# Normalised rows turned by VectorE and DMA instead of TensorE, and row stores issued by ScalarE, in a four-layer float32 block

## The chip, the cores and the metric

The kernel runs on one core of a Trainium2 chip. The metric is the device time of one execution in microseconds. Three executions of the kernel before took 2465.59, 2468.93 and 2472.80 us; the median, 2468.93 us, is the time that the changed kernel is compared with. Engines are named TensorE (PE in the profile), VectorE (DVE), ScalarE (ACT), GpSimd (POOL) and SyncE (SP, which only issues DMAs here).

## The reference

Four layers in a row work on x, 4 batches of 512 rows of 512 numbers, all float32. Each layer adds its result to x:

```python
x = x + attn_a(layernorm(x), Wq, Wk, Wv, Wo)   # "first attention"
x = x + ffn(layernorm(x), w1, w2, w3)          # first feed-forward
x = x + attn_b(layernorm(x), mxfp4 weights)    # "second attention"
x = x + ffn(layernorm(x), w1, w2, w3)          # second feed-forward
```

`layernorm` subtracts the mean of a row and divides by its deviation. First attention has 16 query heads of 128 in 4 groups, each with one key and value head. Its output is half a causal softmax attention with rotary positions, half a gated linear recurrence (`S = S * exp(g) + k v`, with g from the keys). The feed-forward is `sigmoid(n @ q(w1).T) * (n @ q(w2).T) @ q(w3).T`, where n is the normalised x and q rounds weights to -1, 0 and 1. What matters here: every layer begins with normalised rows, and TensorE needs them with the 512 features on partitions, so each block of 128 rows by 512 features has to be turned.

## The kernel before

x stays in SBUF as 16 tiles `xs` of 128 rows. A row block's normalised form is made in `layernorm_steps` (line 123), a Python generator that is advanced from the outer loops, a piece at a time: moments by VectorE (lines 130 to 133), scales (135 to 145, one power on GpSimd), then for each of four row blocks the scaled rows `xn` (line 160, VectorE), four 128x128 transposes by TensorE into one PSUM bank (line 165), and a `sink` that copies the bank to SBUF: ScalarE alone in first attention (line 372), ScalarE and VectorE as a high and a low half in the other layers (`halved`, lines 174 to 177, with `split`, 118 to 121).

First attention (`first_attention_gentle`, line 311) runs 73 steps, one for each 128-row chunk of each of 16 groups (4 batches by 4 head groups) and a few to fill and drain. `step(n)` (line 552) works on several chunks at once, named u to z for chunks n-2 to n+3:

- `A` projects the queries, `B` makes their softmax with decay, turns 32x32 blocks by VectorE (line 461, tile `turned`, one buffer) and stores them to DRAM (line 463); one step later `L` reads them back with the blocks exchanged (line 470), so that queries arrive turned without TensorE.
- `C` turns the rotated queries by TensorE, `D(0)` to `D(3)` make the scores of four heads and their softmax; after the fourth, the turned rows are stored (line 503). `E` reads them back (line 509) at the start of the next step, `own` and `F` form the output, and `G` adds it to x, two steps after the chunk's `D`.
- `part` does the same for the keys of the next group over its four steps p = 0 to 3; `decays` (line 407) sends three one-partition rows `ends` to another place by DMA (line 420).
- `quantise` rounds the feed-forward weights beside all this, a piece at two places of each step.
- `normalise` (line 369) of the next batch is advanced in three of the four steps of the group before it is needed, at up to four places of a step.

In steps 0 to 63 TensorE runs in program order (`manual_schedule`, line 624). The other engines and the rest of the program are ordered by the framework's planner, which puts on each engine what is ready first by its own cost model. `in_place` pins an instruction behind whatever was written before it for the same engine; all these stores and loads are pinned, on SyncE's queue. Each engine then executes its list strictly in order, and a DMA issue that has to wait holds up everything behind it on that engine.

The feed-forward (`feed_forward`, line 1077) loads 11 weight blocks, then for each batch computes 11 pairs of projections (lines 1090 to 1104) and four row blocks of output (1105 to 1112). The next batch's rows are advanced from the loop over blocks (line 1102). Batch 0 of the first feed-forward is normalised during the last steps of first attention (`ahead(50, 0)`, line 1128).

Of the kernel before, what the change touches and what calls it, by code (L numbers as in the profile page):

```python
# [9 lines left out]
F32 = mybir.dt.float32  # L10
# [3 lines left out]
F32R = mybir.dt.float32r  # L14
AF = mybir.ActivationFunctionType
ALU = mybir.AluOpType
# [3 lines left out]
P = 128  # L20
B, S, C = 4, 512, 512
NC = S // P
NK = C // P
# [51 lines left out]
def hybrid_block(ctx: ExitStack, tc: tile.TileContext, a: dict, out: bass.AP):  # L75
# [42 lines left out]
    def split(hi, lo, src, engine=nc.vector):  # L118

        nc.scalar.copy(hi, src)  # L120
        engine.tensor_tensor(lo, src, hi, ALU.subtract)

    def layernorm_steps(b, sink, tag="tp", apart=False, place=lambda i: i):


# [9 lines left out]
        def scales(at):  # L135
# [9 lines left out]
            nc.vector.tensor_tensor(r, r, t, ALU.mult)  # L145

        if not apart:
            for c in range(NC):
                moments(c)
                if c == 1:  # L150
                    yield
            scales(slice(0, NC))
        for c in range(NC):
            if apart:
                moments(c)
                scales(slice(c, c + 1))
            else:
                yield
            xn = lnp.tile([P, C], F32, tag="xn", name="xn", bufs=1)
            nc.vector.tensor_scalar(xn, xs[b * NC + c], mv[:, c, 0:1], rstd[:, c : c + 1], ALU.subtract, ALU.mult)  # L160
            if not apart:
                yield
            tp = bank(tag, [P, NK, P])
            for k in range(NK):
                t = nc.tensor.transpose(tp[:, k, :], xn[:, k * P : (k + 1) * P], ident)  # L165
                if k == 0:
                    place(t)
            sink(c, tp)
# [5 lines left out]
    def halved(pool, b, **kw):  # L174

        halves = [pool.tile([P, NK, S], F32R, tag=f"xn{n}", name=f"xn{n}") for n in ("hi", "lo")]
        return halves, layernorm_steps(b, lambda c, tp: split(*(h[:, :, c * P : (c + 1) * P] for h in halves), tp), **kw)

    def whole(pool, b):
# [130 lines left out]

    def first_attention_gentle(base, extra):

# [5 lines left out]
        with ExitStack() as st:  # L318
# [49 lines left out]

            def normalise(b, apart=False):
                xnT = base.tile([P, NK, S], F32, tag="xnhi", name="xnT")  # L370
                xnTs[b] = xnT
                return layernorm_steps(b, lambda c, tp: nc.scalar.copy(xnT[:, :, c * P : (c + 1) * P], tp), apart=apart)

            class Group:
# [32 lines left out]
                def decays(self):  # L407
# [11 lines left out]
                    for c in range(NC - 1):  # L419
                        nc.sync.dma_start(self.ends[:, c : c + 1], self.down[P - 1 : P, c, :])  # L420
                    n = self.g * B + self.b
# [23 lines left out]
            class Chunk:  # L445
# [9 lines left out]
                def B(self):  # L455
                    c = self.c
                    qd = one.tile([P, HG, D], F32, tag="qd", name="qd")
                    softmax_decayed(qd, self.q_t, lambda h: self.k.down[:, c, :])

                    turned = one.tile([P, 4, HG, 32], F32, tag="turned", name="turned")  # L460
                    nc.vector.transpose(turned.rearrange("p q h t -> p h q t"), qd.rearrange("p h (q j) -> p h q j", q=4))
                    self.queries = dram.tile([P, HG * D], F32, tag="queries", name="queries", bufs=3)
                    in_place(nc.sync.dma_start(self.queries, turned.rearrange("p q h t -> p (q h t)")))
                    self.qr = two.tile([P, HG, D], F32, tag="qr", name="qr")
                    rotate(self.qr, self.q_t, turn[:, c : c + 1, 0:1, :], turn[:, c : c + 1, 1:3, :])

                def L(self):
# [16 lines left out]
                def D(self, h):  # L484
# [15 lines left out]
                    nc.vector.transpose(self.turned.rearrange("p (q h x) -> p q h x", q=4, h=HG)[:, :, h, :], pr.rearrange("p (q x) -> p q x", q=4))  # L500
                    if h == HG - 1:
                        self.passed = dram.tile([P, 4 * HG * P], F32, tag="passed", name="passed", bufs=3)[:, : 4 * HG * 32 * n]
                        in_place(nc.sync.dma_start(self.passed, self.turned))

# [42 lines left out]

            for _ in normalise(0, apart=True):
                pass
            ln = iter(())  # L550
            groups[0] = Group(0, 0)
            def step(n):
                nonlocal ln
                m, p = divmod(n + 7, NC)
                at = lambda i: chunks.get(n + i) if n + i < last else None
                if p == 0 and (m + 2) % KV == 0 and (m + 2) // KV < B:
                    load((m + 2) // KV)
                if (m + 1) % KV == 0 and (m + 1) // KV < B:
                    if p == 1:
                        ln = normalise((m + 1) // KV)  # L560
                    if p > 1:
                        next(ln)
                u, v, w, x, y, z = (at(i) for i in range(-2, 4))
# [4 lines left out]
                if n > -4:  # L568
                    next(quant, None)
                if w:  # L570
                    w.E()
                part(m, p, 0)
# [5 lines left out]
                if x:  # L578
                    x.D(0)
                if z and n > -2:  # L580
                    z.A()
# [3 lines left out]
                if x:  # L585
                    x.D(1)
                if p:
                    next(ln, None)
                if z:
                    z.B()  # L590
                if x:
                    x.D(2)
                if p > 1:
                    next(ln, None)
                if w:
# [14 lines left out]
                if x:  # L610
                    x.D(3)
                if n in (-2, *range(NC + 1, last, NC)):
                    groups[max(n // NC, 0)].load_wo()
                if p:
                    next(ln, None)
                if n > -4:
                    next(quant, None)
                for f in extra.get(n, ()):
                    f()

# [6 lines left out]
            for n in range(last, last + 2):  # L627
                step(n)
            assert next(quant, 0) == 0

# [446 lines left out]
    def feed_forward(base, last, first):  # L1077

        with ExitStack() as st:
# [7 lines left out]
            for b in range(B):  # L1087
                ready, steps = halved(base, b + 1, place=in_place) if b + 1 < B else (None, iter(()))
                hid = []
                for f, (w, _) in enumerate(ws):  # L1090
# [10 lines left out]
                    hid.append(halves)  # L1101
                    for _ in range((f > 1) + (f == 2)):
                        next(steps, None)
                    yield b, f
                for c in range(NC):
                    y = bank("mm", [P, C])
                    project(y, lambda i: hid[i // 2][i % 2][:, c * P : (c + 1) * P], lambda i: ws[i // 2][1][:, 0, :], 2 * NF)
                    x = xs[b * NC + c]
                    nc.vector.tensor_tensor(x, x, y, ALU.add)
                    if last:  # L1110
                        nc.sync.dma_start(x_out[b * NC + c], x)
                    yield b, NF + c
                xn = ready

    with banks(mm=2, sc=3, tp=2, pv=1), tc.tile_pool(name="base", bufs=2) as base:
# [11 lines left out]

        first_attention_gentle(base, ahead(50, 0))
        attention = second_attention_exact(base, ahead(-14, 1))
# [64 lines left out]
```

## Time and profile before

| | before |
|---|---|
| median of three runs | 2468.93 us |
| the profiled execution's own time | 2466.74 us |
| its span, first to last instruction | 2464.8 us |
| busy: TensorE, VectorE, ScalarE, GpSimd | 98%, 67%, 49%, 16% |
| first attention, from the traces | about 0 to 1031 us |
| second feed-forward | about 2194 us to the end |
| TensorE transposes of normalised rows (line 165) | 256, of 280 ns mean |
| DMA, mean over the span | 149 GB/s |

Busy is the union of an engine's instructions. Matmuls are pipelined, so a matmul shown with 0.59 us may follow the one before it after 0.43 us; the distance from start to start is what one costs. The granted clock of TensorE is 0.996 of full speed over the span.

### The profile page before, as it was taken

The numbers are of one execution on the slowest core, as the hardware profiler recorded it, in microseconds if no ns is written. First come the engines' busy times: TensorE is split into PE (matmuls) and PEld (weight loads), VectorE is DVE, ScalarE is ACT, GpSimd is POOL, SyncE is SP. The second block draws the span as 40 slices with busy tenths as digits, with TensorE's granted clock in tenths as the row PEclk, the third lists the DMA queues.
The fourth block names the chain that finished last, engine by engine and source line by source line (L and its number), as shares of the span: only waits on it lengthen the run. The fifth ranks groups of instructions, "written<-read, shape, count | busy, mean of one in ns | idle before, by whom it ended". The sixth has DMA issues, their size and how long they took to land.

```text
span 2464.8 us, 28979 instructions
## 1 busy us (share of the span) xinstructions
PE 2425.2 (98%) x8552; PEld 1543.2 (63%) x8552; DVE 1643.5 (67%) x3816; ACT 1210.8 (49%) x3066; POOL 387.6 (16%) x424
## 2 busy tenths in 40 slices
PE   7999999999999999899999999999999999999998
PEld 4555555555555555488876666666666666658887
DVE  5888777878788888355558676667766666663332
ACT  5666666666666665333336455444444444432221
POOL 1222222222122222022224333100000000000000
PEclk9999999999999999999999999999999999999999
DMA  4667776777656664564536777534343435333000
GB/s 137 198 191 204 201 204 182 205 205 201 180 175 192 196 180 149 193 190 129 143 125 169 199 201 200 144 105 128 91 131 87 132 92 144 78 97 121 18 18 19
DMA packets 240616, 367.11 MB, mean 149 GB/s; under 512 B 41664, under 2 KB 126912, under 8 KB 234304
## 3 DMA queue, kind: packets, MB, share of 16 engines
q1 hardware_dynamic: 214192, 305.03, 44.2%
q10 hardware_dynamic: 18576, 34.95, 4.7%
q0 software_dynamic: 7680, 25.17, 3.6%
q8 instruction: 71, 1.16, 0.2%
q14 instruction: 97, 0.79, 0.1%
HBM read 209.53 MB, written 88.34 MB: 121 GB/s over the span
## 4 chain that ended last, share of the span: by engine, by line
PE 86%; DVE 5%; DMA 3%; issue 2%; ACT 1%; SPq 1%; POOL 1%; DVEq 0%; ACTq 0%; POOLq 0%
PE mm L188 44%; PE sc L188 10%; PE sc L890 8%; PE pv L520 5%; PE sc L490 5%; PE pv L924 4%; PE tp L924 4%; PE sc L480 2%; PE tp L364 2%; PE pv L518 1%; SPq L917 1%; DMA block<-blocks 1%; PE tp L165 1%; DMA prT<-turned 1%; DMA wo<-in_Wo 0%
## 5 line engine op out<-in xcount | busy, mean ns | idle before, releaser
L895 ACT ACTIVATE pr<-sc,nm 128x512 f32<-128x512 f32 x256 | 175.9, 687 | 301.6 <-DVE nm L892 258.3
L188 PE MATMUL sc<-xnhi,block 128*128 128x512 f32 x704 | 278.6, 396 | 3.7 <-ACT hT L1097 2.8
L188 PE MATMUL sc<-xnlo,block 128*128 128x512 f32 x704 | 275.4, 391 | 0.0
L890 PE MATMUL sc<-kT,qT 128*128 128x512 f32 x512 | 262.1, 594 | 0.4 <-ACT kT L872 0.4
L188 PE MATMUL mm<-xnhi,w 128*128 128x512 f32 x512 | 254.4, 497 | 0.0
L188 PE MATMUL mm<-wo,oT 128*128 128x512 f32 x512 | 232.2, 596 | 4.4 <-DMA wo<-in_Wo 3.8
L188 PE MATMUL mm<-wq,xnT 128*128 128x512 f32 x512 | 230.9, 594 | 0.1
L892 DVE TENSOR_REDUCE nm<-sc 128x1 f32<-128x512 f32 x256 | 174.9, 683 | 73.4 <-PE sc L890 70.9
L188 PE MATMUL mm<-xnlo,w 128*128 128x512 f32 x512 | 205.8, 402 | 0.0
L912 DVE STREAM_TRANSPOSE turned<-pr 128x512 f32<-128x512 f32 x256 | 173.4, 696 | 36.8 <-ACT pr L902 34.0
L499 ACT ACTIVATE pr<-pr,den 128x128 f32<-128x128 f32 (+3 forms) x256 | 141.5, 557 | 86.3 <-DVE den L498 84.5
L902 ACT ACTIVATE pr<-pr,den 128x512 f32<-128x512 f32 x192 | 138.2, 722 | 82.3 <-DVE den L900 82.1
L345 POOL TENSOR_TENSOR sw<-q_t,turn 128x256 f32<-128x256 f32 x128 | 97.1, 780 | 495.5 <-ACT q_t L453 396.5
L490 PE MATMUL sc<-krT,qrT 128*128 128x512 f32 (+3 forms) x512 | 170.4, 434 | 0.4 <-DVE own L482 0.4
L497 ACT ACTIVATE pr<-sc,nm 128x128 f32<-128x128 f32 (+3 forms) x256 | 132.9, 520 | 64.0 <-DVE nm L494 54.9
L188 PEld LDWEIGHTS mm<-wo,oT 128*128 128x128 f32 x512 | 96.3, 191 | 105.3 <-issue 95.0
L188 PEld LDWEIGHTS mm<-wq,xnT 128*128 128x128 f32 x512 | 96.3, 191 | 105.1 <-issue 98.8
L500 DVE STREAM_TRANSPOSE turned<-pr 128x128 f32<-128x128 f32 (+3 forms) x256 | 128.4, 503 | 46.7 <-ACT pr L499 43.4
L188 PEld LDWEIGHTS sc<-xnhi,block 128*128 128x128 f32 x704 | 132.8, 189 | 33.3 <-ACT hT L1097 4.0
L188 PEld LDWEIGHTS sc<-xnlo,block 128*128 128x128 f32 x704 | 132.8, 189 | 27.8 <-issue 0.7
L520 PE MATMUL pv<-prT,v_t 128*128 128x512 f32 x320 | 148.0, 592 | 0.0
L890 PEld LDWEIGHTS sc<-kT,qT 128*128 128x128 f32 x512 | 95.8, 189 | 81.4 <-issue 63.6
(151 smaller groups left out, 4800.7 us busy)
## 6 DMA issues: line engine op xcount, KB each, us to landing
prT<-turned SPq DMA_DIRECT2D x1024, 64.0 KB, 2.0
w<-exact SPq DMA_DIRECT2D x32, 1024.0 KB, 5.5
wq<-in_Wq ACTq DMA_DIRECT2D x16, 1024.0 KB, 5.3
queries<-turned SPq DMA_DIRECT2D x64, 256.0 KB, 2.8
qdT<-queries SPq DMA_DIRECT2D x256, 64.0 KB, 3.3
wo<-in_Wo ACTq DMA_DIRECT2D x16, 1024.0 KB, 6.1
passed<-turned SPq DMA_DIRECT2D x16, 1024.0 KB, 4.3
prT<-passed SPq DMA_DIRECT2D x64, 256.0 KB, 5.9
```

What stands on the lines that cost most here:

```text
L188: nc.tensor.matmul(acc, lhsT=lhs(k), rhs=rhs(k), start=k == 0, stop=k == n - 1)
L490: nc.tensor.matmul(sc.rearrange("p q (k j) -> p q k j", j=32), lhsT=self.qrT[:, h, :], rhs=self.k.krT.rearrange("p (k q j) -> p q k j", q= ...
L497: nc.scalar.activation(pr, flat, AF.Exp, bias=nm, scale=-1.0, accum_out=den)
L499: nc.scalar.mul(pr, pr, den)
L500: nc.vector.transpose(self.turned.rearrange("p (q h x) -> p q h x", q=4, h=HG)[:, :, h, :], pr.rearrange("p (q x) -> p q x", q=4))
L520: nc.tensor.matmul(acc.rearrange("p h (a t) -> p h a t", a=4), lhsT=self.k.v_t[:, j, :], rhs=self.wts[:, :, :, j, :], start=j == c == 0, s ...
L890: nc.tensor.matmul(sc, lhsT=qTs[u][:, i * P : (i + 1) * P], rhs=kTs[u], start=True, stop=True)
L892: nc.vector.tensor_reduce(nm, sc, AX.X, ALU.max, negate=True)
L895: nc.scalar.activation(pr, sc, AF.Exp, bias=nm, accum_out=den)
L902: nc.scalar.mul(pr, pr, den)
L912: nc.vector.transpose(turns[u][:, :, i, :], pr.rearrange("p (q k) -> p q k", q=4))
L924: nc.tensor.matmul(accs[u].rearrange("p (n t) -> p n t", t=32), lhsT=v_ts[m, j][:, h * D : (h + 1) * D], rhs=prTs[u].rearrange("p a i (k t ...
```

## The change

Three things change, in first attention and in the second feed-forward.

1. Normalised rows of batches 1 to 3 of first attention, of batch 0 of the first feed-forward, and of batches 1 to 3 of the second feed-forward are no longer turned by TensorE. `to_dram` scales the rows, turns their 32x32 blocks by VectorE and stores 256 KB to DRAM; `from_dram` reads them back by four DMAs of 64 KB that exchange the blocks; ScalarE (and VectorE, for the halves) writes them where the layer reads them. In first attention the turned tile shares the one buffer of `B`'s `turned`, and the tile read back shares the one buffer of `xn`.
2. In first attention the stores of queries and of softmax rows and the three `ends` go from SyncE's queue to ScalarE's, at other places: the rows' store after the next step's `D(0)`, the queries' store after `D(3)`. `E` moves from the start of a step to after `D(1)`.
3. Rows of a batch are advanced at two places of every step over seven steps instead of up to four places over three, starting a few steps earlier; x of a batch is loaded one group earlier. In the second feed-forward the generator is advanced once for every block and output row block.

```diff
+    def to_dram(turned, c, rows):
+        nc.vector.transpose(turned.rearrange("p q k i -> p k q i"), rows(c).rearrange("p (k q j) -> p k q j", k=NK, q=4))
+        passed = dram.tile([P, C], F32, tag="rows", name="rows", bufs=3)
+        in_place(nc.sync.dma_start(passed, turned.rearrange("p q k i -> p (q k i)")))
+        return passed
+
+    def from_dram(back, passed):
+        for q in range(4):
+            in_place(nc.sync.dma_start(back[32 * q : 32 * (q + 1)].rearrange("j (a x) -> j a x", a=4), passed.rearrange("(a j) (q x) -> q j a x", a=4, q=4)[q]))
+        return back.rearrange("p (a k i) -> p k a i", a=4, k=NK)
+
+    def in_halves(halves, c, back):
+        hi, lo = (h[:, :, c * P : (c + 1) * P].rearrange("p k (a i) -> p k a i", a=4) for h in halves)
+        in_place(nc.scalar.copy(hi, back))
+        nc.vector.tensor_tensor(lo, back, hi, ALU.subtract)
+
+    def halved_by_dma(pool, spare, b):
+        halves = [pool.tile([P, NK, S], F32R, tag=f"xn{n}", name=f"xn{n}") for n in ("hi", "lo")]
+        def steps():
+            moments, scales, rows = statistics(b)
...
+            for c in range(NC + 2):
+                yield
+                if c < NC:
+                    passed[c] = to_dram(spare.tile([P, 4, NK, 32], F32, tag="turned", name="turned"), c, rows)
+                yield
+                if 0 < c <= NC:
+                    backs[c - 1] = from_dram(spare.tile([P, C], F32, tag="back", name="back"), passed[c - 1])
+                if c > 1:
+                    in_halves(halves, c - 2, backs[c - 2])
+        return halves, steps()
...
+            def rows_by_dma(b, sink):
+                moments, scales, rows = statistics(b)
...
+                for c in range(NC):
+                    yield
+                    passed = to_dram(one.tile([P, 4, NK, 32], F32, tag="turned", name="turned"), c, rows)
+                    yield
+                    back = from_dram(lnp.tile([P, C], F32, tag="xn", name="back", bufs=1), passed)
+                    yield
+                    sink(c, back)
...
                     for c in range(NC - 1):
-                        nc.sync.dma_start(self.ends[:, c : c + 1], self.down[P - 1 : P, c, :])
+                        in_place(nc.scalar.dma_start(self.ends[:, c : c + 1], self.down[P - 1 : P, c, :]))
...
-                    in_place(nc.sync.dma_start(self.queries, turned.rearrange("p q h t -> p (q h t)")))
+                def store_queries(self):
+                    in_place(nc.scalar.dma_start(self.queries, self.blocks.rearrange("p q h t -> p (q h t)")))
...
-                        in_place(nc.sync.dma_start(self.passed, self.turned))
+                def store_rows(self):
+                    in_place(nc.scalar.dma_start(self.passed, self.turned))
...
+                if p == 0 and (m + 3) % KV == 0 and (m + 3) // KV < B:
+                    load((m + 3) // KV)
                 if p == 0 and (m + 2) % KV == 0 and (m + 2) // KV < B:
-                    load((m + 2) // KV)
-                if (m + 1) % KV == 0 and (m + 1) // KV < B:
-                    if p == 1:
-                        ln = normalise((m + 1) // KV)
-                    if p > 1:
-                        next(ln)
+                    ln = normalise((m + 2) // KV)
...
-                if w:
-                    w.E()
...
                 if x:
                     x.D(0)
+                if w:
+                    w.store_rows()
...
                     x.D(1)
-                if p:
-                    next(ln, None)
+                if w:
+                    w.E()
+                next(ln, None)
...
                     x.D(3)
+                if z:
+                    z.store_queries()
...
-                if p:
-                    next(ln, None)
+                next(ln, None)
...
+                if n == last - 16:
+                    done = halves()
+                    ln = rows_by_dma(0, lambda c, back: in_halves(done, c, back))
...
-                ready, steps = halved(base, b + 1, place=in_place) if b + 1 < B else (None, iter(()))
+                elif last:
+                    ready, steps = halved_by_dma(base, two, b + 1)
...
-                    for _ in range((f > 1) + (f == 2)):
+                    for _ in range(1 if last else (f > 1) + (f == 2)):
                         next(steps, None)
                     yield b, f
                 for c in range(NC):
+                    next(steps, None)
```

## The prediction

> **What bounds the kernel now.** I read the page first (busy shares, slices), then tables of busy time by stretch, TensorE's timeline around the transposes that go, the waits of SyncE's queue, and ScalarE's and SyncE's timelines at the places that get new work.
>
> The page's first part, and the stretches (length, then busy us of TensorE, its weight loads, VectorE, ScalarE, GpSimd; clock; DMA share; GB/s):
>
> ```profile
> PE 2425.2 (98%) x8552; PEld 1543.2 (63%) x8552; DVE 1643.5 (67%) x3816; ACT 1210.8 (49%) x3066; POOL 387.6 (16%) x424
> ```
> ```profile
> 70.00:950.00 880.00, 879.23 (x2806) 481.43 (x2804) 709.16 (x1920) 564.06 (x1729) 193.97 (x207) 1.00 0.67 192
> 950.00:1040.00 90.00, 83.33 (x228) 41.69 (x229) 49.84 (x134) 35.75 (x97) 11.86 (x11) 0.97 0.53 160
> 2195.00:2262.00 67.00, 63.80 (x269) 48.10 (x268) 27.86 (x54) 17.71 (x29) 1.21 (x2) 1.00 0.40 140
> 2300.00:2350.00 50.00, 50.00 (x226) 41.38 (x225) 16.30 (x27) 10.94 (x19) 0.00 (x0) 1.00 0.06 21
> ```
>
> In the body of first attention TensorE is idle for 0.8 of 880 us, at full clock, while VectorE is busy 81% and ScalarE 64%. The second feed-forward is the same with far more room: VectorE 33%, ScalarE 22%, almost no DMA. So an instruction less on TensorE shortens the run by its own distance, as long as what replaces it stays within the cover of the others. TensorE's timeline in both stages:
>
> ```profile
> 657.15 0.39 PE L490 MATMUL sc<-krT,qrT 128*128 128x128 f32 x2
> 657.37 0.60 PE L165 MATMUL tp<-ident,xn 128*128 128x128 f32 x4
> 657.81 0.39 PE L490 MATMUL sc<-krT,qrT 128*128 128x128 f32 x2
> ...
> 2376.09 0.40 PE L188 MATMUL sc<-xnlo,block 128*128 128x512 f32 x1
> 2376.32 0.60 PE L165 MATMUL tp<-ident,xn 128*128 128x128 f32 x4
> 2376.68 0.48 PE L188 MATMUL mm<-block,hhi 128*128 128x512 f32 x1
> 2377.00 0.39 PE L188 MATMUL mm<-block,hlo 128*128 128x512 f32 x1
> 2377.23 0.40 PE L188 MATMUL mm<-block,hhi 128*128 128x512 f32 x1
> ```
>
> The page gives a transpose 280 ns, but starts tell the price: four take 657.81 - 657.37 = 0.44 us, 0.11 each. In the feed-forward they take 0.36, and the matmul after them takes 0.32 where its neighbours take 0.23: 0.45 for a row block.
>
> **What goes.** First attention loses 12 row blocks (batches 1 to 3) and the 4 of the next layer's batch 0, all inside or just behind the stretch without idle: 16 x 0.44 = 7.0 us. The second feed-forward loses 12: 12 x 0.45 = 5.4 us. Together 12.4 us. Less than this can come out, hardly more.
>
> [...]
>
> **What comes in its place.** VectorE: 28 block transposes of 0.68 us (the same shape at line 461: 43.5 us for 64). First attention gets 16, 10.9 us on 709, so 82% busy; its subtractions for the halves read SBUF instead of PSUM, which moves little (line 121: 0.73 against 0.68 us). The copies by ScalarE stay, 0.58 to 0.62 us. SyncE: a row block costs a store and four reads, 0.34 + 4 x 0.43 = 2.1 us of issue by SyncE's timeline (lines 463 and 470); 16 make 33 us, against 176 issues (64 of queries, 64 of rows, 48 `ends`), some 64 us, that leave SyncE. The transfers land as those of the queries do:
>
> ```profile
> queries<-turned SPq DMA_DIRECT2D x64, 256.0 KB, 2.8
> qdT<-queries SPq DMA_DIRECT2D x256, 64.0 KB, 3.3
> ```
>
> 6.1 us for the pair, in a chain spread over seven steps of about 15 us: no reader is near. 28 x 512 KB are 14 MB on 367. I cost all this at nothing; the cover is the 18% that VectorE has left.
>
> **The moves.** The rows' store now waits for the next step's `D(0)`, and `E` is issued behind it. The reads of `E` are used a step later: those of one chunk landed at 529.3 us and `F` began at 540.5, with GpSimd's addition of some 1.7 us between, so several us of delay fit. The queries' store moves behind `D(3)`; its reader `L` is followed by `own` more than a step later. Nothing. But ScalarE now issues 176 DMAs, and it is an engine with work queued behind each: exponentials that free the score banks, copies that TensorE waits for. SyncE's waits before:
>
> ```profile
> SPq L463 <- DVE turned L461: 141.7, 46, 7.3
> SPq L503 <- DVE turned L500: 124.5, 30, 7.4
> SPq L420 <- DMA wq<-in_Wq: 41.5, 5, 8.7
> ...
> SPq L503 <- DMA wq<-in_Wq: 20.7, 3, 8.3
> ...
> SPq L420 <- DMA prT<-passed: 8.1, 12, 1.2
> ```
>
> The first two are waits for VectorE's data, which the later places mostly outlive. The others are stranger: `ends` waits for the landing of transfers that it doesn't use, so DMAs of both queues share completion semaphores. On SyncE that cost nothing; on ScalarE it is a stop. The place is step p = 2:
>
> ```profile
> 540.31 0.63 ACT L417 ACTIVATE down<-held 128x512 f32<-128x512 f32 x1 [0.18 <-DVE held L415]
> ...
> 543.47 0.40 ACT L355 ACTIVATE kd<-k_t,nm 128x128 f32<-128x128 f32 x1 [1.77 <-PE sc L490]
> ...
> 545.84 0.57 ACT L365 COPY qrT<-tp 128x512 f32<-128x512 f32 x1
> ```
>
> Three issues (1.3 us) and the longest wait for `E` (1.2) make 2.5 us, in a place with 1.77 free: 0.7 late. Behind it stand the softmax of the keys, the copies of F and `qrT`; TensorE's `D(0)`, which reads `qrT`, starts at 547.55, 1.1 us after the copy ends. 0.7 fits in 1.1. Bounds for a group: 0, and 8.7 (a full wait for a weight load); I take 0.1, near the first because 12 of the 17 waits are of the short kind: 16 x 0.1 = 1.6 us. In the fill nothing covers them: SyncE needed 1.9 us for the first three, TensorE was waiting on this chain; between 0 and 1.9 I take 1.3.
>
> The shared buffer `turned` can hold VectorE: `B` must wait until the row block's store has landed, or the row block until the queries' store has. Bounds 0 and 2.8 us for each of 16; before, line 461 had no idle in front. VectorE late by 2.8 us still frees a score bank in time (three banks, five uses in a step of about 15 us, so some 9 us until reuse). I take 0.
>
> The second feed-forward's start has a row that matters:
>
> ```profile
> 2214.95 13.89 SPq L264 DMA_DIRECT2D block<-blocks  x18
> ```
>
> The first row store stands behind these and can't go before 2228.8. With the 7.6 us of a block's landing it frees its buffer at about 2236.5; the third row block wants it after block 5, at about 2218.6 + 4 x 3.63 = 2233.1 (block 2's first matmul starts at 2218.6; 16 matmuls of 0.227). VectorE could stand still for 3.4 us with the gate products behind it, while TensorE has one bank, half a block, ahead. Between 0 and 3.4 I take 1.0, because the planner may have other work in front.
>
> **Sum.** -7.0 - 5.4 + 1.6 + 1.3 + 1.0 = -8.5 us. On the profiled execution (2466.74) 2458.2; the median of the runs shown is 2.2 above it, so 2460.4 us, 0.34% faster. About 0.3% (7.4 us) is what a measurement can tell from no change.
>
> **Rivals.**
> - ScalarE becomes the stop: slower. `E`'s later store makes its landings later, and the `ends` wait for them. For it: the shared semaphores, the 5 waits for weight loads, only 1.1 us until `D(0)`. Against it: the waits for `E` were 0.7 us on average. Without my 1.6 the sum is -10.1, so it breaks even at 0.63 us of TensorE idle in each of 16 groups, and is 0.3% slower at 1.1. At 1.5 it gives 2468.9 - 10.1 + 24 = 2482.8.
> - `turned` holds VectorE and TensorE runs dry in the 28 steps with rows: first attention's 7.0 us are lost, 2467.4. For it: VectorE is busy without a break over several us in such steps. Against it: the banks.
> - The second feed-forward's start takes the full 3.4: 2462.8.
>
> That the transposes stay is excluded by the code.
>
> **How the numbers follow.** Forecast 0.52, of which 0.49 are beyond 0.3%; its own range is 2454 to 2462 (all 12.4 kept, some us of run spread; or the small costs doubled). ScalarE's stop 0.22, `turned` 0.16, the start 0.10. Faster 0.49 + 0.01 of the last; same 0.03 + 0.16 + 0.08; slower 0.22 + 0.01. For 8 in 10 I leave out the worst half of ScalarE's case and a little below: 2453 to 2483.
>
> **What would show it.** Line 165 with 144 transposes instead of 256; TensorE's starts 0.44 closer at the row blocks; idle of TensorE between 70 and 940 us still near 0.8. The forecast is wrong if `D(0)` (line 490) or `own` gets idle time released by ScalarE in steps p = 2 and 3, if line 461 has idle in front that a DMA ends, or if VectorE stands at 2233 for a buffer.

## The result, and the profile after

| | before | after |
|---|---|---|
| median (6 runs each, side by side) | 2469.25 us | 2492.11 us |
| lowest and highest | 2465.59, 2472.80 | 2488.34, 2497.43 |
| the profiled execution's own time | 2466.74 us | 2496.31 us |
| its span | 2464.8 us | 2494.5 us |

The ratio is 1.0097, 95% interval 1.0082 to 1.0112: 0.97% slower, 22.9 us by the medians. The forecast was 2460.4 us, 8.5 us faster, with 2483 as the upper end of its range. The two profiled executions lie 29.6 us apart, more than the medians, because before's is 2.5 us under its median and after's 4.2 us over. The page of the profile after opens with almost the same busy times as before:

```profile
PE 2425.4 (97%) x8440; PEld 1533.9 (61%) x8440; DVE 1638.5 (66%) x3844; ACT 1211.3 (49%) x3066; POOL 379.9 (15%) x424
```

TensorE has 112 matmuls fewer and the same busy time in a span 30 us longer. Where that went is read from the first matmul of the same kind in both traces (`own` of chunk 1, 8, 52 and 62, counted from 0, the last `G`, the last score of second attention, the output rows of the second feed-forward; the differences are of unrounded times):

| stretch | before | after | difference | forecast |
|---|---|---|---|---|
| start to `own` of chunk 1 (fill) | 73.3 | 80.8 | +7.5 | +1.3 |
| chunk 1 to 8 | 103.8 | 104.6 | +0.8 | -5.4 for this and the next three |
| chunk 8 to 52 (body) | 680.9 | 694.5 | +13.6 | |
| chunk 52 to 62 | 138.1 | 143.7 | +5.7 | |
| chunk 62 to the last `G` (drain) | 38.2 | 42.4 | +4.2 | |
| to the last score of second attention | 1152.3 | 1153.3 | +1.0 | 0 |
| to the first output row, second feed-forward | 66.7 | 68.8 | +2.1 | -0.8 |
| to its last matmul | 203.5 | 199.5 | -4.0 | -3.6 |

The stretches of the profile after, in the columns of the table in the prediction:

```profile
70.00:950.00 880.00, 857.87 (x2692) 465.65 (x2691) 676.78 (x1896) 553.64 (x1700) 181.31 (x201) 1.00 0.67 197
950.00:1070.00 120.00, 107.75 (x288) 51.99 (x288) 64.94 (x174) 52.08 (x142) 16.86 (x17) 0.96 0.50 151
2300.00:2350.00 50.00, 50.00 (x223) 41.39 (x222) 21.99 (x34) 14.76 (x26) 0.00 (x0) 1.00 0.17 57
```

The body had 0.8 us of idle time in 880; it has 22.1 (880 - 857.87). VectorE and ScalarE are not busier in it than before (677 against 709 us, 554 against 564), so no engine became the bound by its load. TensorE's waits in the profile after (stretch 70 to 940 us: in total, times, longest) say what it stood for. The first line is the whole list of before in this stretch, the others are the longest of after:

```profile
PE mm L188 <- DVE x L193: 0.2, 1, 0.2
PE mm L239 <- DVE held L485: 13.9, 10, 2.7
PE tp L416 <- ACT krT L500: 2.4, 1, 2.4
PE mm L239 <- DVE state L512: 2.3, 2, 1.9
PE mm L239 <- DVE gatelo L121: 1.5, 1, 1.5
```

Ten waits for `held`, at one place of the program. It is `G`, in steps p = 2. TensorE and VectorE before (first fence) and after (second) there:

```profile
535.29 0.79 PE L188 MATMUL mm<-gatehi,until 128*128 128x512 f32 x1
535.93 0.40 PE L188 MATMUL mm<-gatelo,until 128*128 128x512 f32 x1
536.16 3.60 PE L188 MATMUL mm<-wo,oT 128*128 128x512 f32 x8
539.61 0.67 DVE L415 TENSOR_SCALAR held<-mm 128x512 f32<-128x512 f32 x1
```

```profile
549.09 0.79 PE L239 MATMUL mm<-gatehi,until 128*128 128x512 f32 x1
549.72 0.39 PE L239 MATMUL mm<-gatelo,until 128*128 128x512 f32 x1
552.82 3.70 PE L239 MATMUL mm<-wo,oT 128*128 128x512 f32 x8 [2.71 <-DVE held L485]
552.09 0.68 DVE L485 TENSOR_SCALAR held<-mm 128x512 f32<-128x512 f32 x1
```

`gatehi` and `gatelo` sum the decays into the bank `dec`, and `held` (VectorE) reads it. `G` has nothing to do with either. Before, it started 0.23 us after `gatelo` and `held` came 3.5 us later: `held` was late there already, and nothing on TensorE waited for it. After, `G` starts only when `held` has ended. That is what it looks like when `G` has been given the PSUM bank of `dec`, one of the two of the pool `mm`, instead of the bank that the copy `q_t` frees. By the semaphores in the traces, `G` behind `gatelo` waits for ScalarE in all 14 groups where it stands there before, and for VectorE in 10 of these 14 after.

SyncE's queue after, in the same stretch:

```profile
SPq L542 <- DMA queries<-turned: 277.8, 46, 11.6
SPq L194 <- DVE turned L192: 45.9, 6, 9.3
SPq L582 <- DMA passed<-turned: 44.1, 18, 6.0
```

SyncE no longer waits for VectorE's softmax rows; it reaches its reads early and waits for the stores that ScalarE issues. In the drain this lets something else run ahead. Before (first fence) and after (second):

```profile
995.26 0.38 ACTq L390 DMA_DIRECT2D wo<-in_Wo  x1
997.32 0.34 SPq L503 DMA_DIRECT2D passed<-turned  x1
997.76 0.85 SPq L264 DMA_DIRECT2D block<-blocks  x2
1000.65 5.33 PE L188 MATMUL mm<-wo,oT 128*128 128x512 f32 x8 [3.52 <-DMA wo<-in_Wo]
```

```profile
1020.94 1.79 SPq L315 DMA_DIRECT2D block<-blocks  x4
1022.87 0.39 ACTq L460 DMA_DIRECT2D wo<-in_Wo  x1
1032.32 5.49 PE L239 MATMUL mm<-wo,oT 128*128 128x512 f32 x8 [7.58 <-DMA wo<-in_Wo]
```

Before, the first two loads of feed-forward blocks stood on SyncE behind the rows' store of 997.3 us and left at 997.8, after Wo (995.3); Wo landed in 5.3 us. After, four of them, 1.5 MB, leave 2 us before the last Wo, which lands 9.4 us after its issue, and `G` waits 7.58 us for it instead of 3.52. The four blocks land 6.2 and 7.0 us after their issues (medians of the 512 KB and the 256 KB ones), so they are in flight beside Wo; whether they delay it is asked in experiment 8.

The 5.7 us from chunk 52 to 62 have two stops in front: 1.91 us for `state` at 895.3 and 1.87 us for Wo at 977.0. Behind each, TensorE runs at half clock for a while (granted 0.50 from 896.1 to 899.3 and from 978.0 to 981.2 us; 128x512 matmuls start 0.85 us apart instead of 0.43); the granted clock over this stretch is 0.98, where before has 1.00.

### The profile page after: what moved, and what is told of

Read it like the earlier page. It is cut to its first block, busy times and chain, and to the rows that moved or that the text cites. A ratio compares the mean times of both kernels' runs of the same rounds, so it can differ in the third digit from the quotient of the medians.

```text
span 2494.5 us, 28914 instructions
## 1 busy us (share of the span) xinstructions
PE 2425.4 (97%) x8440; PEld 1533.9 (61%) x8440; DVE 1638.5 (66%) x3844; ACT 1211.3 (49%) x3066; POOL 379.9 (15%) x424
## 4 chain that ended last, share of the span: by engine, by line
PE 84%; DVE 6%; DMA 4%; issue 2%; ACT 1%; POOL 1%; SPq 1%; ACTq 0%; DVEq 0%; POOLq 0%
PE mm L239 43%; PE sc L239 9%; PE sc L961 8%; PE pv L593 5%; PE sc L562 5%; PE tp L995 4%; PE pv L995 4%; PE sc L552 2%; PE tp L416 1%; PE pv L591 1%; DMA block<-blocks 1%; SPq L988 1%; DMA wo<-in_Wo 1%; DMA raw<-in_wq_scales 1%; DMA raw<-in_wo_scales 1%
## 5 line engine op out<-in xcount | busy, mean ns | idle before, releaser
L239 PE MATMUL mm<-wo,oT 128*128 128x512 f32 x512 | 235.1, 602 | 24.1 <-DVE held L485 13.9
```

The costliest lines, as they stand in the source:

```text
L239: nc.tensor.matmul(acc, lhsT=lhs(k), rhs=rhs(k), start=k == 0, stop=k == n - 1)
```

## The experiments

The table gives each kernel's ratio to the kernel before, measured beside it, and TensorE's idle time from two places of its profile: the sum of its waits from 70 to 940 us, and the wait of `G` for the last group's Wo.

| kernel | ratio (95%) | waits 70 to 940 | wait for Wo |
|---|---|---|---|
| before | 1 | 0.2 us | 3.5 us |
| after | 1.0097 (1.0082 to 1.0112) | 22.1 | 7.6 |
| 1: rows' store on SyncE | 1.0260 (1.0241 to 1.0279) | 42.4 | 6.9 |
| 2: decays in the other banks | 1.0046 (1.0031 to 1.0060) | 17.4 | 7.1 |
| 3: before, rows' store by ScalarE | 1.0116 (1.0091 to 1.0142) | 19.7 | 6.6 |
| 4: before, second feed-forward | 0.9966 (0.9955 to 0.9977) | 0.9 | 3.6 |
| 5: before, queries and `ends` by ScalarE | 1.0053 (1.0037 to 1.0069) | 9.3 | 3.7 |
| 6: as 2, rows by TensorE | 1.0049 (1.0033 to 1.0065) | 11.9 | 7.0 |
| 7: as 4, rows in own space, nothing moved | 0.9978 (0.9969 to 0.9988) | 7.1 | 3.6 |
| 8: as 2, blocks behind E | 1.0060 (1.0044 to 1.0075) | 15.9 | 3.4 |
| 9: as 2, rows in own space | 1.0060 (1.0045 to 1.0076) | 13.9 | 6.7 |
| 10: as 7, x two steps later | 1.0011 (1.0002 to 1.0020) | 9.8 | 3.4 |
| 11: before, x one group earlier | 1.0002 (0.9992 to 1.0011) | 2.5 | 3.7 |
| 12: before, `ends` by ScalarE | 1.0007 (0.9997 to 1.0018) | 2.6 | 3.7 |

**1. The rows' store back on SyncE.**

```diff
-                    in_place(nc.scalar.dma_start(self.passed, self.turned))
+                    in_place(nc.sync.dma_start(self.passed, self.turned))
```

> The changed kernel with one edit: the rows' store (64 DMAs) is issued by SyncE again, at its new place after the next step's D(0). Theory 'bank' (in steps p = 2 the planner gives G's output the PSUM bank of the decays, so that G waits for VectorE's `held`, and it does so since the rows' store went to ScalarE's queue): the wait of G for `held` is gone, the step p = 2 takes 13.6 us again instead of 14.8, and the body of first attention gives back its 14.4 us of loss and the 5.25 us of gain that was due: about 2492 - 20 = 2472 us. Rival 'issues' (ScalarE is held by the DMAs that it issues and by what they wait for): 64 of 176 issues leave ScalarE, so about a third of the same 20 us comes back: about 2485 us, with the wait for `held` still there.

2535.94 us. The wait for `held` went as the theory has it, and yet the kernel is slower than the one it was to mend, 1.026 of before against 1.0097. Three of TensorE's waits from 70 to 940 us:

```profile
PE pv L593 <- DMA prT<-passed: 20.6, 3, 9.7
PE pv L593 <- DMA qdT<-queries: 5.7, 1, 5.7
PE mm L239 <- DVE held L485: 0.4, 1, 0.4
```

SyncE and TensorE in this kernel:

```profile
115.44 1.73 SPq L542 DMA_DIRECT2D qdT<-queries  x4
...
117.69 0.43 SPq L576 DMA_DIRECT2D passed<-turned  x1
125.28 0.32 SPq L194 DMA_DIRECT2D rows<-turned  x1
126.17 1.93 SPq L582 DMA_DIRECT2D prT<-passed  x4
136.01 2.90 PE L593 MATMUL pv<-prT,v_t 128*128 128x512 f32 x3 [9.74 <-DMA prT<-passed]
```

The last softmax rows of this chunk were turned at 104.2 us. Their store leaves SyncE only at 117.7, because the reads of `L` stand in front and wait for the queries' store, which ScalarE issued at 113.4 and which landed at 115.4; in the changed kernel the same store left ScalarE at 107.0. It lands at 124.1. Behind it the store of a normalised row block waits until 125.3 for VectorE, which itself stood still for the shared buffer `turned` until the next queries' store had landed at 124.5. Only then do the reads of `E` leave, the last landing at 135.9. `F` stops for 9.74 us. From 70 to 940 us such waits for `prT` and `qdT` add up to 26 us. So the parts of the change lean on each other: with the queries' store on ScalarE and the normalised rows on SyncE, the softmax rows' store can't go back to SyncE's queue without harm.

**2. The decays' sums in the other pair of banks.**

```diff
-                    dec = bank("mm", [P, NC, D])
+                    dec = bank("tp", [P, NC, D])
```

> The changed kernel with one edit: the sums of `decays` are written to the pair of PSUM banks of the transposes instead of the pair that G and the projections use; all 176 DMAs stay on ScalarE. Theory 'bank': G no longer waits for `held`; about 2472 us, as with the store on SyncE, or up to 5 us more if transposes now wait for the bank. Rival 'issues': nothing that holds ScalarE is changed, 2490 to 2494 us. This is the run that tells the two apart.

2483.88 us, half way. `G` starts behind `gatelo` again, with all 176 DMAs still on ScalarE (TensorE's timeline):

```profile
552.42 0.79 PE L239 MATMUL tp<-gatehi,until 128*128 128x512 f32 x1
553.05 0.39 PE L239 MATMUL tp<-gatelo,until 128*128 128x512 f32 x1
553.28 3.16 PE L239 MATMUL mm<-wo,oT 128*128 128x512 f32 x7
```

The wait for `held` belongs to the bank, not to ScalarE. But the body (chunk 8 to 52) takes 686.1 us, 8.4 less than after and still 5.2 more than before: 6.8 us of other idle time in it, for `state`, `gatelo`, `gatehi`, scores and Wo.

**3. Before, with only the rows' store moved to ScalarE and `E` behind D(1).**

```diff
-                    if h == HG - 1:
...
-                        in_place(nc.sync.dma_start(self.passed, self.turned))
+                def store_rows(self):
...
+                    in_place(nc.scalar.dma_start(self.passed, self.turned))
...
-                if w:
-                    w.E()
...
                     x.D(0)
+                if w:
+                    w.store_rows()
...
                     x.D(1)
+                if w:
+                    w.E()
```

> The kernel before with one part of the change: the rows' store by ScalarE after the next step's D(0), and E behind D(1). All normalised rows by TensorE, queries and `ends` by SyncE. Theory 'bank': the wait of G for `held` appears in 13 of 14 steps p = 2 at about 1.2 us each: 2469 + 16 = 2485 us. Rival 'issues': 64 of 176 issues, a third of 20 us: about 2476 us, spread over all steps. A third theory, 'rows' (VectorE and the DMAs of the normalised rows delay the body): none of them is here, 2469 us.

2499.06 us: this part alone costs the kernel before as much as the whole change does (1.0116 and 1.0097, with intervals that overlap). The wait that it brings, first in total (us, times, longest) and then at one of its longest places, in TensorE's timeline:

```profile
PE mm L188 <- DVE held L415: 17.4, 13, 2.0
```

```profile
486.80 0.40 PE L188 MATMUL mm<-gatelo,until 128*128 128x512 f32 x1
489.18 5.40 PE L188 MATMUL mm<-wo,oT 128*128 128x512 f32 x8 [1.98 <-DVE held L415]
```

It comes in 13 groups. The eight matmuls of `G` behind this wait take 5.40 us instead of 3.60: the first of them start 0.85 us apart instead of 0.43, and the granted clock from 489.2 to 494.6 us is 0.68. So this wait cost 3.8 us, not 2. The body took 19.2 us more than before, 14.0 of them idle.

**4. Before, with the second feed-forward's part alone.**

```diff
-                ready, steps = halved(base, b + 1, place=in_place) if b + 1 < B else (None, iter(()))
...
+                elif last:
+                    ready, steps = halved_by_dma(base, two, b + 1)
...
```

> The kernel before with the second feed-forward's part of the change alone. The prediction's terms: -5.4 us for 12 row blocks, +1.0 at its start: 2465 us. Theory 'start' (read from the changed kernel's trace: 1.8 us gained for each of three batches, but 3.9 us lost at the start, in waits for the last rows of second attention and in matmuls at a lower clock after them): about 2467.5 us; the loss at the start may also not come at all, if it was made further ahead, then 2463.7.

2464.08 us, 0.34% faster than before, the lowest ratio of the study. From its first matmul to its last the second feed-forward takes 257.1 us instead of 262.9, 5.8 less. The loss at the start is not there.

**5. Before, with the queries' store and `ends` by ScalarE.** (The same moves as in the change, without the rows' store.)

> The kernel before with the queries' store (behind D(3)) and the three `ends` issued by ScalarE; the rows' store, E and all normalised rows as before. 112 of the 176 issues are on ScalarE. Theory 'bank': without the rows' store G doesn't wait for `held`, so the body (chunk 8 to chunk 52, 680.9 us before) is the same within 1 us; the fill pays for `ends`, some 4 us until the second chunk's own product; the drain is as before, since SyncE is still held up by the rows' store and so lets no weight block run ahead of the last Wo: 2469 + 4 = 2473 us. Rival 'issues': 112 issues cost two thirds of 20 us in the body as well, 2486 us.

2484.51 us, between the two theories and nearer to "issues". There is no wait for `held`, so the bank theory holds for what it says of that wait; its time does not. The fill took 4.0 us more than before and chunk 52 to 62 another 5.7, with a wait of 3.04 us for Wo in it; the body took 687.3 us, 5.9 of it idle, in eight places with six different causes (`state`, `pr`, `xnT`, `x`, `q_t`, Wo), none over 1.5 us.

**6. As 2, with the normalised rows of first attention and of the first feed-forward's batch 0 by TensorE.**

> The changed kernel with the decays' sums in the other pair of banks and the normalised rows of first attention (and of the first feed-forward's batch 0) by TensorE again, at the changed kernel's places; all moved DMAs on ScalarE, second feed-forward changed. It asks what is left of the body's loss once the bank is mended (10.5 us more than forecast between chunk 8 and chunk 52). Theory 'rows' (VectorE waits for the shared buffer `turned` and then reaches `state`, `gatelo` and the exponentials' inputs late): no rows here, so the body takes 681 to 682 us, and the whole 2464 (second feed-forward alone) + 4 (fill) + 4 (drain) = 2472 us. Rival 'moves' (the moved stores hold it without the bank too): the body stays at 686 + 5 (transposes back) = 691 us, the whole 2489.

2482.75 us. Theory "rows" fell: without any row by DMA the body takes 692.9 us, 8.6 of it idle. It isn't the same idle time, though: 6.2 us are one stop that experiment 2 doesn't have, at 360.9 us, where ScalarE has the cast of `gatehi` behind the scaling of a softmax row that waits for a reciprocal, and VectorE has that reciprocal behind the sum of a rotation and a maximum for the next keys. TensorE's two longest waits in the stretch 70 to 940 us:

```profile
PE tp L239 <- ACT gatehi L120: 6.2, 1, 6.2
PE tp L416 <- ACT krT L498: 2.4, 1, 2.4
```

**7. Nothing moved, rows in space of their own.**

```diff
+                space = base.tile([P, NK, S], F32, tag="xnlo", name="space")
...
+                for c in range(NC + 2):
+                    yield
+                    ...              # read back row block c - 1, copy c - 2, turn c into space[:, c % 2]
+                    yield
+                    if c < NC:
+                        passed[c] = dram.tile([P, C], F32, tag="rows", name="rows", bufs=3)
+                        in_place(nc.sync.dma_start(passed[c], turned))
```

> The kernel before with the second feed-forward's part, and with the normalised rows of batches 1 to 3 and of the first feed-forward's batch 0 by VectorE and DMA, but no store of queries, rows or `ends` is moved and E stays where it was. The rows have space of their own (turned and read-back tiles in the part of SBUF that the feed-forward's low halves use later), one row block a step: read back and turned at the first place of a step, stored at the second, so that no issue waits for data just made. If the transposes are worth the prediction's 0.44 us each and the loss came from the moves and the shared buffer: 2464 - 7 = 2457 us, body 675.6 us between chunk 8 and chunk 52. If rows by VectorE and DMA cost in themselves (VectorE's time, SyncE's 10 more issues in a step behind which the reads of E stand): 2464 us or more.

2466.51 us: faster than before, but not than the feed-forward's part alone. The body took 679.9 us: the 36 transposes of this stretch are gone (3.9 us by the distances of their starts), and its idle time has risen from 0.5 to 2.7 us. The fill lost 2.8 us, and the start of the second feed-forward takes 2.7 us longer than in experiment 4.

**8. As 2, the first weight blocks pinned behind the last `E`.**

```diff
-            nc.sync.dma_start(w.bitcast(F32), blocks[f, :, at : at + n, :])
+            load = nc.sync.dma_start(w.bitcast(F32), blocks[f, :, at : at + n, :])
+            if hold:
+                in_place(load)
...
```

> The changed kernel with the decays' sums in the other banks (2483.9 us) and one more edit: the first feed-forward's first two weight blocks are pinned on SyncE behind the last reads of E, so that they are no longer in flight when the last Wo is loaded. Theory 'drain' (with the rows' store off its queue SyncE lets four block loads go 2 us before the last Wo, which then takes 9 us to land instead of 5): the wait of G for Wo before the last chunk falls from 7.1 to about 3.5 us and the second-last chunk to last G from 42 to 38 us: about 2480 us. Rival (Wo is late for another reason, such as its own issue on ScalarE): the wait stays at 7 us, 2484.

TensorE's and SyncE's timelines of this kernel in the drain:

```profile
1018.50 5.40 PE L239 MATMUL mm<-wo,oT 128*128 128x512 f32 x8 [3.39 <-DMA wo<-in_Wo]
1036.41 2.07 SPq L315 DMA_DIRECT2D block<-blocks  x4
```

The blocks leave 23 us after Wo (issued at 1013.2), which lands in 5.2 us, and chunk 62 to the last `G` takes 35.4 us instead of 41.9. So the cause of the long wait is shown. In the whole time it doesn't show: the ratio is 1.0060 against 1.0046 without this edit, on another chip and with intervals that overlap.

**9. As 2, rows in space of their own, stores still moved.** (Experiment 7's generator in experiment 2's kernel.)

> The changed kernel with the decays' sums in the other banks, and with the rows in space of their own, one row block a step, stored by SyncE half a step after they are turned. The moved stores stay on ScalarE. It asks whether the shared buffer `turned` is behind the 6.3 us of idle time that the body keeps with the bank mended. Theory 'turned': VectorE no longer waits for the queries' store in front of a row's block transposes, TensorE's waits for `state` and `gatelo` go with it, the body takes 686 - 5 = 681 us: about 2479 us. Rival 'order' (each version gets another order of VectorE's and ScalarE's work, and TensorE meets other late inputs, whatever the buffer): some 4 to 8 us of idle time in other places, 2482 to 2487 us.

2483.21 us. In the changed kernel VectorE stood still for the shared buffer six times, 6.2 us in all, 3.0 at the longest. Here none of it is left, and TensorE's idle time in the body went up, from 6.8 to 9.7 us, in other places (`gatelo` 4.7, `pr` 1.8, `gatehi` 1.7, `state` 1.5). The rival "order" gave the number. The order of the work differs from experiment 2's, too, so what the wait for the buffer costs by itself is not shown.

**10. As 7, x of a batch loaded two steps later.**

```diff
-                if p == 0 and (m + 3) % KV == 0 and (m + 3) // KV < B:
+                if p == 2 and (m + 3) % KV == 0 and (m + 3) // KV < B:
```

> The version with nothing moved and the rows in their own space (2466.5 us), with one edit: x of a batch is loaded two steps later, so that batch 1's four row blocks are not fetched during the fill. Theory: the fill's 2.8 us (the second chunk's own product at 76.1 instead of 73.3 us) come from the earlier load, which the change has too; they go, and 2463.7 us are left, the body as before at 680 us. Rival: the fill's loss is one of order and stays, 2466.5 us, or goes to another place.

2471.82 us, a ratio of 1.0011 against experiment 7's 0.9978: the theory fell. The fill got worse (chunk 1's `own` at 78.4 us) and the body too, by one stop in another place, for GpSimd's sum in `F`:

```profile
PE pv L599 <- POOL prT L594: 5.5, 1, 5.5
```

**11. Before, with x one group earlier and nothing else.**

```diff
-                if p == 0 and (m + 2) % KV == 0 and (m + 2) // KV < B:
-                    load((m + 2) // KV)
+                if p == 0 and (m + 3) % KV == 0 and (m + 3) // KV < B:
+                    load((m + 3) // KV)
```

> The kernel before with one edit that adds and removes no work: x of a batch is loaded one group earlier, as in the change. Rows by TensorE, all stores by SyncE. The transfers are long done either way, but the order of VectorE's and ScalarE's work comes out different in many places. Theory 'order' (the kernel before has an order in which TensorE meets no late input, 0.5 us of idle time between chunk 8 and chunk 52; any other order has some): 2 to 8 us of idle time in the body and up to 5 in the fill, 2469 + 6 = 2475 us. Rival (a new order as such costs nothing, it is the moved DMAs and the rows that cost): 2469 us, 1 us of idle time in the body.

2471.35 us beside 2471.46: no difference. In the body the idle time rose from 0.5 to 2.7 us, the low end of what "order" allowed. So this new order made TensorE wait a little by itself, too little to be told from nothing in the time.

**12. Before, with `ends` by ScalarE and nothing else.**

> The kernel before with the three `ends` of each group issued by ScalarE, and nothing else; the order of the other engines is nearly that of before. The prediction's terms: 1.3 us in the fill and 0.1 in each of 16 groups, 2.9 in all: 2472 us. By the traces of the other versions with `ends` on ScalarE the wait of TensorE for `kd` in the fill is 2.1 to 3.6 us instead of under 1, and matmuls at half clock follow it: 3 to 4 us in the fill; the body as before if the order is what costs there: 2473 us. If ScalarE's issues cost in the body as well (0.6 us for each of the three, 44 groups' chunks): 5 us more, 2478.

2473.36 us, 1.9 more than before beside it, not distinguishable from none. In the body nothing (680.5 us, 0.4 idle): three issues in each group cost TensorE nothing there. Chunk 52 to 62 took 3.5 us more, with one wait of 2.06 us for Wo in it; experiment 11, without these issues, has the same wait (1.93), and before has not. In the fill the issues do cost. ScalarE, VectorE and TensorE there, before and in this kernel:

```profile
30.57 0.61 ACT L417 ACTIVATE down<-held 128x512 f32<-128x512 f32 x1
31.47 0.62 ACT L422 ACTIVATE held<-held 128x512 f32<-128x512 f32 x1
32.26 1.60 DVE L358 SCALAR_TENSOR_TENSOR kd<-kd,den,held 128x128 f32<-128x128 f32 x4
32.66 0.48 PE L364 MATMUL tp<-ident,kd 128*128 128x128 f32 x1
```

```profile
30.36 0.61 ACT L417 ACTIVATE down<-held 128x512 f32<-128x512 f32 x1
31.00 0.52 ACTq L420 DMA_DIRECT2D ends<-down  x1
31.57 1.27 ACTq L420 DMA_DIRECT2D ends<-down  x2
32.88 0.63 ACT L422 ACTIVATE held<-held 128x512 f32<-128x512 f32 x1 [1.52 <-issue]
35.13 0.69 DVE L346 TENSOR_TENSOR qr<-qr,sw 128x512 f32<-128x512 f32 x1 [1.58 <-POOL sw L345]
35.74 1.13 DVE L358 SCALAR_TENSOR_TENSOR kd<-kd,den,held 128x128 f32<-128x128 f32 x4
36.14 0.48 PE L364 MATMUL tp<-ident,kd 128*128 128x128 f32 x1 [3.64 <-DVE kd L358]
```

The three issues stand between the two exponentials, and the second starts 1.4 us later. That is the smaller part: with `held` due later, VectorE's order now has two sums of rotations in front of `kd`, which wait for GpSimd, so `kd` starts 2.2 us after `held` is ready, and TensorE's first transpose of it 3.5 us later than before. Chunk 4's `own` comes at 118.3 us instead of 113.9.

## Why the prediction was wrong

**The terms for what goes were right.** The page after has 144 transposes at line 175 instead of 256. The prediction had 0.11 us for one; in the body 36 are worth 3.9 us. In the second feed-forward a row block was worth 0.48 us, where the prediction had 0.45: 1.9 us less from one batch's first output row to the next, for each of the two such stretches with rows, and 5.8 us for the whole part alone against 5.4 forecast. VectorE's added 0.71 us per block (line 192, median of 28; the prediction had 0.68) and SyncE's issues did not make either the bound.

**The step that failed is the moves' "Nothing", and with it "I cost all this at nothing; the cover is the 18% that VectorE has left".** They took every instruction's place in its engine's order, and the PSUM bank that it gets, as they were before. The rows' store with `E` behind it (experiment 3) brings the wait of `G` for `held`, and the bank alone (experiment 2) takes it away: 13.9 us of waits from 70 to 940 us, and 0.51 of the 0.97% in time. Why the planner gives `G` this bank once the store is moved was not looked into. The wait was in no row of the trace of before, since it did not exist there; but what it is made of was: `held` ended some 4 us after `gatelo`, beside an engine that had 0.8 us of idle time in 880. No work was added: a result that was late and harmless became one that somebody waits for.

**The rival "ScalarE becomes the stop" had the place and nearly the price, with the wrong mechanism.** It named steps p = 2 and 1.1 us a group for 0.3% slower, and the waits for `held` came to about 1.4 us in each of 10 groups. That the price was close is luck. But the wait is `G`'s, not `D(0)`'s, and VectorE ends it. Experiment 12 shows ScalarE's `ends` to be harmless in the body, as the 0.1 us a group had them. The range left out "the worst half" of this case, and that is where the time is.

**The fill was mis-sized.** 1.3 us between 0 and 1.9, from the time of the three issues; they delay ScalarE by 1.4, but `kd` by 3.5 us, because VectorE's order shifts with them, and chunk 4 by 4.4 (experiment 12). `ends` alone cost 3.3 us at chunk 1 (experiment 12). After has 7.5 us there, with more waits of 2.0 to 2.6 us.

**The drain was not in the forecast.** SyncE's long waits for VectorE, which the prediction called waits that "the later places mostly outlive", had also kept the weight blocks back. That is 4.2 us in the profile; holding the blocks back again took 6.5 us off this stretch (experiment 8), which did not show in the whole time.

**`turned` as a cost of its own was not seen.** VectorE does wait for it, 6.2 us in all, in front of the rows' transposes (line 192) and not of the queries', where the prediction had looked for it; but the kernel without the wait is no faster (experiment 9 against 2: 1.0060 and 1.0046). In experiment 1 the same buffer held VectorE for 1.05 us in the chain behind a stop of TensorE.

**The second feed-forward's start** lost 2.9 us against the forecast, not by the predicted stall: at 2275.85 us VectorE turns the third row block without idle time before it. TensorE waited 1.95 us for the last `prT` of second attention, where before waited 0.96, and the granted clock there was 0.50 from 2237.5 to 2244.1 us, 0.95 from 2227 to 2290. With the part alone (experiment 4) that wait is 0.94 and nothing is lost, so it isn't the second feed-forward's rows. All seven kernels of this study in which first attention's rows go by DMA have 1.5 to 2.5 us there, and all seven others 0.9 to 1.2. What ties the two together stays open.

**What stays open.** With the bank mended 7 to 10 us of idle time remain in the body. As much is there without the rows (6) and without the shared buffer (9), but at other places each time, so these two are not excluded as a part of it. `ends` alone bring none (12), and the order as such brought only 2 us where it was tried alone (11). The queries' store by ScalarE with `ends` has 5.9 (5), in small pieces at changing places. Whether that store or the orders that it leads to are the cause was not separated. Nor was it tried to carry out the change with the order of before. The stop for Wo between chunk 52 and 62 has no cause yet either.

## What to carry to other kernels

Where the bound engine has next to no idle time, ask of every edit who will be given the buffers and banks that are freed, and which late result next to it is harmless today; an edit that takes work off the engine can lose more by that than it gains. Try the parts of a change alone: here the part far from any tight order gained 0.34% by itself, and moving one store, with the reads behind it, cost as much as the whole change. A queue that waits a lot may be pacing someone: before its waits are removed, look at what stands behind them.

## What the runs showed of the hardware

Some gaps of TensorE cost twice here. At a granted clock of 1.00 a 128x512 matmul of `G` starts 0.43 us after the one before; behind some gaps it is 0.85 us for a while. Behind the wait of 1.87 us in the changed kernel the granted clock was 0.50 from 978.0 to 981.2 us. The wait of 1.98 us in experiment 3 (line at 489.18) was followed by such matmuls, with a granted clock of 0.68 over the eight; the wait of 2.71 us in the changed kernel (552.82: 3.70 us for eight) was not, with 1.00. In first attention behind 100 us, gaps of the changed kernel and of experiment 3 up to 1.7 us were never followed by it; of nine between 1.8 and 2.8 us five were; the two of 6.6 and 7.6 us were. The length alone does not tell them apart: in the changed kernel 1.87 us before eight matmuls of `G` (977.03) was followed by it, 5.40 us for the eight at a granted clock of 0.68, and 1.86 us before another eight (804.84) was not, 3.70 us at 1.00. What decides it is not shown.
